# Splitting a projection by columns over two interleaved stages of a four-layer vision kernel

## Chip, cores and metric

The kernel runs on one core of a Trainium2 chip, as one program. The metric is the device time of one execution in microseconds. The time before is 5893.0 us, the median of three runs (5887.95 to 5899.55).

## What is computed

The input x has the shape (8, 56, 56, 192), in float32 throughout. Four layers follow each other, each of the form x = x + layer(groupnorm(x)). Layers 0 and 1 are alike and are the ones that matter here; layer 2 is a depthwise convolution with an MLP, layer 3 a windowed attention. Cut to what matters, with w for the layer's own weights:

```python
x = gn(x)                                  # (8, 56, 56, 192), normalized in 32 groups
p = silu(x @ p_w.T + p_b)                  # 576 channels
q = silu(x @ q_w.T + q_b)
v = silu(x @ v_w.T + v_b)
qv = q * v
o1 = toeplitz(qv along w, a1)              # per channel, a 56 x 56 Toeplitz matrix
o2 = toeplitz(qv along h, a2)
out = (p * (o1 + o2)) @ o_w.T + o_b        # back to 192 channels, added to x
```

The Toeplitz matrices a1 and a2 come from a small MLP over the lags, times a decay. The reference computes these products by FFT; the kernel multiplies by the matrices.

## The kernel before

Samples are held in pairs (j and j + 4), so that there are four pairs; j0 = 0 names the pairs 0 and 1, j0 = 2 the pairs 2 and 3. Each of layers 0 and 1 is made of three generators for each j0:

- Q(i, j0), `tno_qv` (from L223): the projection to q and v, 1152 columns in all, their Silu and their product qv. It walks over 3136 tokens in groups of 256: `load` (L235, issued at L239 on SP's queue) fetches x of two groups ahead, `normalize` (L242, L245 on ScalarE) applies the group norm in place. Each block of 128 tokens is taken against columns 0 to 511, 512 to 1023 and 1024 to 1151 in turn (the loop over c0). `unit` (L253) makes the matmuls (L262), in which x is the loaded weight and the columns of wq move, and adds the bias on VectorE (L271). One unit later `multiply` (L296) makes the Silu (L300, ScalarE) and the product of the q and v halves (L303, GpSimd); its store to qv in HBM (L306, SP's queue) is issued one `multiply` later still. The columns are laid out in blocks of 128, of which the first 64 are q channels and the next 64 the v channels that belong to them, so that column c0 yields the block rows from 2 * c0 / 128 of qv.
- TZ(i, j0), `tno_toeplitz` (from L364): 9 pairs of block rows of qv, each taken along w (d = 0) and along h (d = 1), so 18 rounds. A round loads its part q of qv (L378 or L381) and its matrices tm (L388), both on SP's queue and both double buffered, and makes 8 groups of matmuls (L401), each copied out of PSUM by ScalarE (L408). VectorE transposes (L419, L421), GpSimd adds the second direction (L423) and stores the sum o (L433). The load of round n + 2 is issued at the end of round n. It gives 72 steps of two groups.
- O(i, j0), `tno_out` (from L473): the gate p, its product with o, the output projection, the residual and the statistics of the next group norm. It walks over 28 tiles of 224 tokens of a pair: loads of x (L119) and of o (L498, the tile `t<-L_sum`), normalization (L505), matmuls for p (L526, L535, L561, L563), Silu (L545), the gate on GpSimd (L552, L581), the output matmuls (L568 to L576), residual (L584, L587), a store (GpSimd's queue) and statistics (L590).

The tiles of Q and O come from the same pools, tp with three buffers of each kind: t6 holds x, t8 the projection's result z or O's s, t4 products. Every group of matmuls takes one of four PSUM tiles (`bank`).

The order of the work is written out by hand: within the Toeplitz stages the instructions of every compute engine stand in the order in which the Python code makes them (`manual_schedule`). `weave` (L628) makes that order. It runs a lane, a list of generators each with a cost, one after the other; each yield returns the cost that was just issued. Beside it it draws steps of a Toeplitz generator so that their share of the cost `given` follows the lane's progress:

```python
want = (done / total - lo) / (hi - lo) * given
while steps is not None and gave < want:
    more = next(steps, None)
```

with lo = 0.04 and hi = 0.92. When 0.9 of a generator's cost is done, `weave` starts the first loads of the one that follows; before it starts those of the next weave's lane it draws what is left of the steps. The costs are QT = 298.1 for a Q, OT = 299.6 for an O and TZT = 238.4 for a TZ.

`tno_layers` (L665) lists the lanes at L720 and L721 and runs them in four Toeplitz weaves at L731 and L732:

| weave | lane | Toeplitz steps | from to, us |
|---|---|---|---|
| 1 | Q(0, 2) | TZ(0, 0) | to about 1050 |
| 2 | O(0, 0), Q(1, 0) | TZ(0, 2) | 1050 to 1888 |
| 3 | O(0, 2), Q(1, 2) | TZ(1, 0) | 1888 to 2722 |
| 4 | O(1, 0) | TZ(1, 2) | 2722 to 3297 |

Afterwards O(1, 2) runs beside the first half of layer 2's convolution (L735). The weights wq of Q live in a pool of their own, wqp, which is closed after the third weave.

Of the kernel before, what the change touches and what calls it, by code (L numbers as in the profile page):

```python
# [31 lines left out]
D1 = 576  # L32
# [6 lines left out]
def view(ap, offset, dims):  # L39

    return bass.AP(ap.tensor, ap.offset + offset, [ap.ap[0], *dims])


class Net:
# [175 lines left out]
        for more in self.all_norms():  # L220
            pass

    def tno_qv(self, L, j0, xs, gn, qv, apart=None):  # L223

# [8 lines left out]
        def load(g):  # L235
            t0, n = g * GT, min(GT, T - g * GT)
            x = p.tile([128, 2, 3, GT], F32, name="t6")
            of = xs[j0 : j0 + 2, :, :, t0 : t0 + n].rearrange("j k p t -> p (j k) t")
            nc.sync.dma_start(x[:, :, :, :n].rearrange("p j k t -> p (j k) t"), of)  # L239
            return x, t0, n  # L240

        def normalize(x, t0, n, js=(0, 1)):  # L242
            for j in js:
                for k in range(3):
                    nc.scalar.activation(  # L245
                        x[:, j, k, :n],
                        x[:, j, k, :n],
                        AF.Identity,
                        bias=gn[:, j0 + j, k, 1:2],
                        scale=gn[:, j0 + j, k, 0:1],  # L250
                    )

        def unit(x, s, m, c0, n, z):  # L253


            pps = [(c, min(256, n - c), self.bank2()) for c in range(0, n, 256)]
            for part in range(2):
                for c, k, pp in pps:
                    for j in range(2):
                        for b in range(2):  # L260
                            rows = HALF[b] if part else slice(0, 128)
                            nc.tensor.matmul(  # L262
                                pp[:m, b, 256 * j : 256 * j + k],
                                x[rows, j, 2 if part else b, s : s + m],
                                w[rows, part, c0 + c : c0 + c + k],

                                start=part == 0 and j == 0,
                                stop=part == 1 and j == 1,
                            )
            for c, k, pp in pps:  # L270
                nc.vector.tensor_add(  # L271
                    z[:m, c : c + k, :],
                    view(pp[:m], 0, [[1, k], [256, 4]]),
                    view(bias[:m], c0 + c, [[1, k], [0, 4]]),
                )
# [20 lines left out]
        def multiply(m, n, z, at, c0):  # L296
            k = n // 128
            for f in stores:
                f()
            nc.scalar.activation(z[:m, :n, :], z[:m, :n, :], AF.Silu)  # L300
            prod = p.tile([128, 4, DC * 4], F32, name="t4")
            half = z[:m, :n, :].rearrange("p (n h c) b -> p n h (c b)", h=2, c=DC)
            nc.gpsimd.tensor_mul(prod[:m, :k], half[:, :, 0], half[:, :, 1])  # L303
            n0 = c0 // 128
            stores[:] = [
                lambda: nc.sync.dma_start(  # L306
                    qv[2 * n0 : 2 * n0 + 2 * k, at : at + m, :].rearrange("n t e -> t n e"),
                    prod[:m, :k].rearrange("p n (h e) -> p (n h) e", h=2),
                )
            ]  # L310

        stores = []
        groups = -(-T // GT)
# [4 lines left out]
        if apart:  # L318
            units = []
            for g in range(2):  # L320
                x, t0, n = loaded[g]
                for s in range(0, n, 128):
                    for c0 in range(0, 2 * D1, 512):
                        k = min(512, 2 * D1 - c0)
# [19 lines left out]
        for g in range(2 if apart else 0, groups):  # L344
            x, t0, n = loaded.pop(0)
            for s in range(0, n, 128):
                m = min(128, n - s)
                for c0 in range(0, 2 * D1, 512):
                    k = min(512, 2 * D1 - c0)

                    if late is not None:
                        multiply(*late)
                    if c0 == 512 and s + 128 >= n and g + 1 < groups:
                        normalize(*loaded[0])
                    z = p.tile([128, 512, 4], F32, name="t8")
                    unit(x, s, m, c0, k, z)
                    late = (m, k, z, t0 + s, c0)
                    if c0 == 0 and s == 0 and g + 2 < groups:
                        loaded.append(load(g + 2))
                    yield 5.3 * k / 512  # L360
        multiply(*late)
# [303 lines left out]
    def tno_layers(self, x0, x1, x2, gn, last):  # L665


        tc, nc = self.tc, self.nc
        LS = ("L0", "L1")
        tables = [  # L670

            [self.dram.tile([D1 + 1, 112], F32, name=f"{L}_tab{d}") for d in range(2)]
            for L in LS
        ]
        mats = [
            [self.dram.tile([D1 // 32, 64, 32 * H], F32, name=f"{L}_mat{d}") for d in range(2)]
            for L in LS
        ]
        qvs = {

            j0: self.dram.tile([D1 // 32, 64 * W, 128], F32, name=f"qv{j0}") for j0 in (0, 2)
        }
        o = [self.dram.tile([B // 2, 9, 128, T], F32, name=f"{L}_sum") for L in LS]
        x = (x0, x1, x2)
        with ExitStack() as ctx, ExitStack() as wqp:
            self.wqp = wqp.enter_context(tc.tile_pool(name="wqp", bufs=1, side="right"))
            self.tp = ctx.enter_context(tc.tile_pool(name="tp", bufs=3))
            Q = lambda i, j0, apart=None: self.tno_qv(LS[i], j0, x[i], gn[i], qvs[j0], apart)
            O = lambda i, j0, woven=True: self.tno_out(LS[i], j0, x[i], gn[i], o[i], x[i + 1], gn[i + 1], woven)
            TZ = lambda i, j0: self.tno_toeplitz(j0, mats[i], qvs[j0], o[i])  # L690
            QT, OT, TZT = 25 * 2.25 * 5.3, 28 * 10.7, 8 + 72 * 3.2

            with tc.tile_pool(name="tab", bufs=2) as tab:
                stats = [self.input_stats(x0, gn[0], j, tab) for j in range(4)]
                for more in stats[0]:
                    pass
                first = Q(0, 0, tab)
                next(first)

                for n in range(14):  # L700
                    next(first)
                    next(stats[1], None)
                for more in stats[1]:
                    pass
                for n in range(10):
                    next(first)
                self.decay_tables("L0", tab, tables[0])
                for st in stats[2:]:
                    for more in st:
                        next(first)  # L710
                none = tab.tile([112, 512], F32, name="none", bufs=1)
                nc.gpsimd.memset(none, 0.0)
                for qv in qvs.values():
                    to = qv[:, T:].rearrange("n (p k) e -> p n (k e)", p=112)
                    nc.gpsimd.dma_start(to, view(none, 0, [[0, D1 // 32], [1, 512]]))
                self.decay_tables("L1", tab, tables[1])
                for t in tables:
                    for d in range(2):
                        nc.gpsimd.dma_start(t[d][D1:], none[:1, :112])
                lanes = [[(first, QT - 104.0)], [(Q(0, 2), QT)], [(O(0, 0), OT), (Q(1, 0), QT)]]  # L720
                lanes += [[(O(0, 2), OT), (Q(1, 2), QT)], [(O(1, 0), OT)], [(O(1, 2, False), OT)]]  # L721
                mat = (m for i in range(2) for m in self.expand_tables(tables[i], mats[i]))
                self.weave(lanes[0], mat, lanes[1][0][0], 72.0, 0.0, 0.88)
            in_order = tc.manual_schedule(engines=ENGINES)
            with tc.tile_pool(name="tz", bufs=1) as self.tz, in_order:
                self.tms = []
                for i in range(2):
                    tm = self.tz.tile([128, 32 * H + 8], F32, name=f"tm{i}")
                    nc.gpsimd.memset(tm, 0.0)
                    self.tms.append(tm)  # L730
                for n, tz in enumerate((TZ(0, 0), TZ(0, 2), TZ(1, 0), TZ(1, 2))):  # L731
                    self.weave(lanes[n + 1], tz, lanes[n + 2][0][0], TZT)  # L732
                    if n == 2:
                        wqp.close()
            self.weave(lanes[5], **last())  # L735


# [906 lines left out]
```

## Time and profile before

| | us |
|---|---|
| median of three runs | 5893.0 |
| the profiled execution | 5873.81 |
| its span, from the first to the last instruction | 5872.0 |
| TensorE busy | 5361.4 (91%) |
| VectorE busy | 2362.3 (40%) |
| ScalarE busy | 2267.0 (39%) |
| GpSimd busy | 2209.1 (38%) |
| mean TensorE clock granted | 0.955 |

All lines shown are of that one execution. L262 is line 262 of the kernel. In the page's slices a digit is the busy share of one fortieth of the span in tenths, PEclk is the granted clock of TensorE in tenths of full speed, and DMA is the mean busy share of the 16 DMA engines. In tables by stretch each line gives the stretch, its length, and then for each engine the busy time and in brackets the number of instructions, followed by clock, DMA share and GB/s. In the timeline a line is a run of like instructions: start, length from the first's start to the last's end, engine, line, operation, what is written and read, how many, and in square brackets the engine's idle time before it with what ended it. The hardware records each float32 matmul of the kernel as two. PEld is the weight load, SPq the DMA queue of SP.

### The profile page before, as it was taken

Reading aid. Unit: us, or ns where it says so; the run is one execution under the profiler, and the core shown is the slowest. Engines: PE = TensorE matmul, PEld = TensorE weight load, DVE = VectorE, ACT = ScalarE, POOL = GpSimd, SP = SyncE. Lnnn points to the kernel's source line nnn. Section 1 sums busy time; section 2 is a strip of 40 time slices with the busy share of each in tenths; the row PEclk is TensorE's granted clock in tenths of the full one; section 3 lists DMA queues with packets and bytes.
Section 4 is the critical chain, followed back from the end, with each engine's and each line's share of the span. In section 5 each row is a group of like instructions: output and inputs, shape, how many; then the busy total and the mean of one; then the engine's idle time right before and its main releaser. Section 6 shows DMA issues by size and latency. Waiting matters only on the chain.

```text
span 5872.0 us, 143924 instructions
## 1 busy us (share of the span) xinstructions
PE 5361.4 (91%) x64672; PEld 3891.5 (66%) x64672; DVE 2362.3 (40%) x3770; ACT 2267.0 (39%) x2990; POOL 2209.1 (38%) x1529
## 2 busy tenths in 40 slices
PE   5998888899999999999888799989999999889897
PEld 2776666677777777777666678856665445666665
DVE  6434454233454233553344322331222322555565
ACT  2334454344454444554444322242323333333332
POOL 1334566466456565565666300000001001333332
PEclk8999998999999999999999899999999999999998
DMA  7799997788786788886999566634444223344442
GB/s 267 162 220 264 268 280 238 222 257 273 209 234 213 238 251 230 242 256 191 310 287 303 171 210 207 231 123 155 149 161 120 65 62 62 73 96 84 92 88 59
DMA packets 1139528, 1119.25 MB, mean 191 GB/s; under 512 B 342528, under 2 KB 1076736, under 8 KB 1123488
## 3 DMA queue, kind: packets, MB, share of 16 engines
q1 hardware_dynamic: 1103328, 909.05, 56.8%
q0 software_dynamic: 35584, 200.98, 8.9%
q8 instruction: 508, 8.32, 0.6%
q14 instruction: 108, 0.88, 0.1%
HBM read 753.79 MB, written 389.15 MB: 195 GB/s over the span
## 4 chain that ended last, share of the span: by engine, by line
PE 54%; DMA 11%; POOL 10%; issue 8%; DVE 8%; SPq 6%; ACT 3%; POOLq 0%; DVEq 0%; ACTq 0%
PE bank L262 12%; PE bank L953 6%; POOL s L423 4%; PE bank L814 4%; PE bank L1033 4%; PE bank L401 4%; DMA qv<-t 4%; PE bank L526 4%; PE bank L571 3%; DMA t<-L_sum 3%; PE bank L1047 3%; SPq L378 2%; POOL t L552 2%; SPq L388 2%; POOL t L303 2%
## 5 line engine op out<-in xcount | busy, mean ns | idle before, releaser
L262 PE MATMUL bank<-wq,t 128*128 128x256 f32 (+4 forms) x7680 | 1308.2, 379 | 101.4 <-DVE t L271 50.8
L262 PEld LDWEIGHTS bank<-wq,t 128*128 128x128 f32 (+2 forms) x7680 | 1021.3, 193 | 391.4 <-issue 113.3
L271 DVE TENSOR_TENSOR t<-bank,wq 128x1024 f32<-128x1024 f32 (+3 forms) x480 | 517.3, 1112 | 821.3 <-PE bank L262 559.1
L303 POOL TENSOR_TENSOR t<-t 128x1024 f32<-128x1024 f32 (+2 forms) x288 | 518.9, 1815 | 728.5 <-DMA qv<-t 395.4
L408 ACT COPY ot<-bank 128x896 f32<-128x896 f32 x576 | 492.7, 914 | 643.2 <-PE bank L401 377.1
L423 POOL TENSOR_TENSOR s<-s,ot 128x1568 f32<-128x1568 f32 x144 | 617.9, 4296 | 78.4 <-DVE ot L421 77.7
L401 PE MATMUL bank<-q,tm 56*32 56x224 f32 x18432 | 515.3, 359 | 72.4 <-DMA tm<-L_mat 23.1
L300 ACT ACTIVATE t<-t 128x2048 f32<-128x2048 f32 (+2 forms) x288 | 422.7, 1488 | 407.3 <-DVE t L271 393.1
L401 PEld LDWEIGHTS bank<-q,tm 56*32 56x32 f32 x18432 | 348.8, 107 | 203.8 <-issue 121.0
L552 POOL TENSOR_TENSOR t<-t,t 128x896 f32<-128x896 f32 x168 | 347.2, 2084 | 344.3 <-DMA t<-L_sum 164.3
L526 PE MATMUL bank<-t,wo 128*128 128x224 f32 x1792 | 394.8, 375 | 51.3 <-ACT t L505 22.7
L584 DVE SCALAR_TENSOR_TENSOR t<-bank,wo,t 128x448 f32<-128x448 f32 x112 | 76.4, 682 | 885.7 <-ACT t L580 417.3
L953 PE MATMUL bank<-z,w 128*128 128x448 f32 (+1 forms) x1344 | 417.5, 558 | 3.4 <-ACT h L962 3.4
L526 PEld LDWEIGHTS bank<-t,wo 128*128 128x128 f32 x1792 | 348.2, 201 | 88.5 <-issue 28.6
L545 ACT ACTIVATE t<-bank,wo 128x448 f32<-128x448 f32 x448 | 248.0, 635 | 396.9 <-PE bank L535 368.4
L571 PE MATMUL bank<-t,wo 128*128 128x224 f32 x1792 | 376.2, 364 | 0.0
L127 POOL DMA_DIRECT2D x<-x x64 | 36.7, 573 | 870.1 <-DVE x L984 840.0
L571 PEld LDWEIGHTS bank<-t,wo 128*128 128x128 f32 x1792 | 335.8, 193 | 33.0 <-issue 31.7
L814 PEld LDWEIGHTS bank<-xt,cm 113*112 113x112 f32 x3072 | 314.8, 180 | 45.6 <-issue 38.3
L419 DVE STREAM_TRANSPOSE s<-ot 128x1792 f32<-128x1792 f32 x144 | 292.3, 2034 | 112.2 <-DMA L_sum<-s 65.0
L814 PE MATMUL bank<-xt,cm 113*112 113x108 f32 (+2 forms) x3072 | 326.0, 266 | 8.3 <-ACT h L962 5.1
L953 PEld LDWEIGHTS bank<-z,w 128*128 128x128 f32 (+1 forms) x1344 | 183.7, 190 | 209.6 <-issue 200.2
(149 smaller groups left out, 6984.4 us busy)
## 6 DMA issues: line engine op xcount, KB each, us to landing
q<-qv SPq DMA_DIRECT2D x36, 3584.0 KB
q<-qv SPq DMA_DIRECT2D x72, 1568.0 KB
L_sum<-s POOLq DMA_DIRECT2D x288, 392.0 KB, 7.4
t<-L_sum SPq DMA_DIRECT2D x112, 1008.0 KB
qv<-t SPq DMA_DIRECT2D x192, 512.0 KB
cm<-in_L_cm SPq DMA_DIRECT2D x96, 896.0 KB
tm<-L_mat SPq DMA_DIRECT2D x72, 896.0 KB
x<-t POOLq DMA_DIRECT2D x112, 336.0 KB, 7.1
```

What stands on the lines that cost most here:

```text
L262: nc.tensor.matmul(pp[:m, b, 256 * j : 256 * j + k], x[rows, j, 2 if part else b, s : s + m], w[rows, part, c0 + c : c0 + c + k],  start=p ...
L271: nc.vector.tensor_add(z[:m, c : c + k, :], view(pp[:m], 0, [[1, k], [256, 4]]), view(bias[:m], c0 + c, [[1, k], [0, 4]]),)
L300: nc.scalar.activation(z[:m, :n, :], z[:m, :n, :], AF.Silu)
L303: nc.gpsimd.tensor_mul(prod[:m, :k], half[:, :, 0], half[:, :, 1])
L401: nc.tensor.matmul(pt[32 * j : 32 * j + 32, r, hf * 224 : (hf + 1) * 224], tm[rows, at : at + 32], q[rows, :, 4 * c : 4 * c + 4], start=Tr ...
L408: nc.scalar.copy(view(ot, 4 * (g % 4), [[16, 2], [32, 112], [1, 4]]), view(pt, 0, [[512, 2], [4, 112], [1, 4]]),)
L423: nc.gpsimd.tensor_add(to, to, view(of, 0, [[1, 28], [32, 56]]))
L526: mm(gs[c // 2][:, b, c % 2 * 256 : c % 2 * 256 + N], pw[:, 0, 128 * c : 128 * c + 128], xn[:, b], start=c % 2 == 0, stop=False,)
L552: gate.tensor_mul(to, to, pg)
L571: mm(P[:, b, :N], ow[:, c, 0:128], g[:, 4 * b + c], start=False, stop=c == 3 and b == 1)
L814: nc.tensor.matmul(pc[:, 128 * e + 4 * m0 : 128 * e + 4 * m1], cm[:113, e, k, :], xt[:, m0 - 1 + k : m1 - 1 + k, c + e, :], start=n == 0 a ...
L953: nc.tensor.matmul(phs[c][:, s, :TT], w0[rows, part, at : at + 128], z[rows, Z[2 if part else s], :], start=part == flip, stop=part != flip,)
```

## The change

`tno_qv` gets a range of columns. Its loop over c0 runs over that range only, the place of the normalization of the next group and of the load of the next but one are set by the range, and all else stays. The projection of the second layer for the pairs 2 and 3, Q(1, 2), is made of two generators. The first takes the columns 0 to 511 of all tokens and stays in the third weave, behind O(0, 2). The second takes the columns 512 to 1151, and stands at the head of the fourth weave's lane, ahead of O(1, 0). It loads and normalizes x again. The fourth weave's Toeplitz products TZ(1, 2) are drawn from its beginning, so that their first rounds, on the block rows 0 to 7 of qv, stand beside the second pass, whose own block rows are 8 to 17. The costs given to `weave` are 4/9 and 5/9 of QT. The pool of wq is closed after the fourth weave.

```diff
-    def tno_qv(self, L, j0, xs, gn, qv, apart=None):
+    def tno_qv(self, L, j0, xs, gn, qv, apart=None, cols=(0, 2 * D1)):
...
-                for c0 in range(0, 2 * D1, 512):
-                    k = min(512, 2 * D1 - c0)
+                for c0 in range(*cols, 512):
+                    k = min(512, cols[1] - c0)
...
-                    if c0 == 512 and s + 128 >= n and g + 1 < groups:
+                    if c0 == max(cols[0], min(512, cols[1] - 512)) and s + 128 >= n and g + 1 < groups:
                         normalize(*loaded[0])
...
-                    if c0 == 0 and s == 0 and g + 2 < groups:
+                    if c0 == cols[0] and s == 0 and g + 2 < groups:
                         loaded.append(load(g + 2))
...
-            Q = lambda i, j0, apart=None: self.tno_qv(LS[i], j0, x[i], gn[i], qvs[j0], apart)
+            Q = lambda i, j0, *more: self.tno_qv(LS[i], j0, x[i], gn[i], qvs[j0], *more)
...
-                lanes += [[(O(0, 2), OT), (Q(1, 2), QT)], [(O(1, 0), OT)], [(O(1, 2, False), OT)]]
+                parts = [Q(1, 2, None, cols) for cols in ((0, 512), (512, 2 * D1))]
+                lanes += [[(O(0, 2), OT), (parts[0], QT * 4 / 9)], [(parts[1], QT * 5 / 9), (O(1, 0), OT)]]
+                lanes += [[(O(1, 2, False), OT)]]
...
                     self.weave(lanes[n + 1], tz, lanes[n + 2][0][0], TZT)
-                    if n == 2:
-                        wqp.close()
+                wqp.close()
```

## The prediction

> **What bounds the kernel now.** I read the page's slices first, then cut the timeline at the weaves' boundaries and looked at busy times stage by stage, then at what TensorE waited for, and last at single instructions to get prices.
>
> ```profile
> PE   5998888899999999999888799989999999889897
> PEclk8999998999999999999999899999999999999998
> DMA  7799997788786788886999566634444223344442
> ```
>
> PE is nearly full everywhere, but slices 20 to 22 (2.8 to 3.2 ms) show PE at 8 and DMA at 9: there the transfers hold TensorE back. In the third weave (1888 to 2722 us, output projection O(0,2) and projection Q(1,2) beside the Toeplitz products TZ(1,0)) and the fourth (2722 to 3297 us, O(1,0) beside TZ(1,2)):
>
> ```profile
> core 0: us, PE busy (x) PEld busy (x) DVE busy (x) ACT busy (x) POOL busy (x), PEclk, DMA share, GB/s
> 1888.00:2722.00 834.00, 802.32 (x8899) 616.35 (x8898) 334.81 (x356) 384.64 (x527) 483.07 (x295) 0.98 0.80 236
> 2722.00:3297.00 575.00, 486.72 (x6872) 368.08 (x6872) 205.98 (x226) 240.33 (x374) 364.99 (x226) 0.93 0.93 279
> ```
>
> The third is TensorE's: 96% busy, clock 0.98, DMA with room. The fourth is not: TensorE idles 88 us and its granted clock is 0.93. Cut into three:
>
> ```profile
> 2722.00:2750.00 28.00, 20.65 (x120) 16.18 (x120) 0.68 (x1) 10.29 (x17) 11.94 (x7) 0.82 0.98 202
> 2750.00:3230.00 480.00, 423.83 (x6492) 320.50 (x6496) 188.83 (x199) 216.59 (x334) 303.33 (x191) 0.95 0.97 294
> 3230.00:3297.00 67.00, 42.23 (x280) 31.41 (x259) 16.47 (x26) 13.44 (x24) 49.72 (x29) 0.82 0.58 205
> ```
>
> For 480 us DMA stands at 0.97, so that stretch goes at the transfers' pace; before it lies a start in which O fills its pipeline, after it a tail with no Toeplitz work. Prices come from undisturbed places in the timeline:
>
> ```profile
> 2689.65 32.28 PE L262 MATMUL bank<-wq,t 128*128 128x256 f32 x206
> ...
> 2735.27 6.27 PE L526 MATMUL bank<-t,wo 128*128 128x224 f32 x16 [7.35 <-ACT t L505]
> ...
> 2771.47 3.26 PE L401 MATMUL bank<-q,tm 56*32 56x224 f32 x128
> 2774.65 3.29 PE L526 MATMUL bank<-t,wo 128*128 128x224 f32 x16
> ...
> 2788.32 3.26 PE L401 MATMUL bank<-q,tm 56*32 56x224 f32 x128
> 2791.50 3.10 PE L526 MATMUL bank<-t,wo 128*128 128x224 f32 x15
> ```
>
> From L526 to L526 is 16.85 us with three Toeplitz steps (192 L401 records). A step (64 records) costs 1.6 us (3.18 from start to start for two), so an output tile costs 12.0. 206 records of L262 take 32.28 us; a block of 128 tokens has 80, so 12.5 us; the 512-column part is 32 of its 72 record weights (a 128-wide record counted half), 5.6 us, the other 640 columns 6.9.
>
> **What the Trainium skill says.** "Perfetto Trace Analysis", Optimization Strategy: where a kernel has regimes with different most-contended engines, interleaving them may help. The trace has such regimes, 0.80 and 0.93 of DMA. "TensorE: Matmul & The Clock Gate", What's actually happening: after about 3.4 us of idling the array's clock is gated to half. The trace agrees: after 7.35 us idle, 16 matmuls take 6.27 us, against 3.29 at 2774.65. So a stall costs more than its length. "DMA: Bandwidth & Descriptors", Issuing engines are not separate DMA queues: transfers of SP and POOL share the same 16 engines; so the new loads add to one budget. The 0.97 above is of all queues together, which fits; no run here isolates it.
>
> **The change, part by part.** Work per stage at those prices. O and TZ: 28 tiles x 12.0 + 72 steps x 1.6 = 451 us of TensorE. Q: 25 blocks x 12.5 = 313. So the third weave holds 764 and takes 834 (70 lost), the fourth holds 451 and takes 575 (124 lost).
> DMA, as share times length: fourth 0.93 x 575 = 535 for O and TZ; third 0.80 x 834 = 667, so Q costs 132. Q moves 9.6 MB of x and 28.9 MB of stores; by bytes 33 and 99.
>
> (1) Moved: the 640-column pass, 25 x 6.9 = 174 us of TensorE, from the third weave to the fourth, with its DVE adds, Silus, POOL products, 50 of 75 stores. TensorE after: third 451 + 139 = 590, fourth 451 + 174 = 625. POOL would be 0.6 busy in each, as it is now in the fourth (365/575 = 0.63): not a bound.
> (2) Added: 13 loads of x on SP's queue (9.6 MB) and 78 normalizations (L245) on ACT. 78 of them take 38.67 us in the third weave, so 39 us on an ACT that stays under 0.5 busy. They hide behind TensorE; if the cover is gone they hold back the Silus and PSUM copies behind them. DMA after: third 535 + 33 + 99 x 4/9 = 612; fourth 535 + 33 + 99 x 5/9 = 623.
> (3) Re-dealt: Toeplitz steps. The weave spreads 238 units of cost over 432 instead of 598 in the third, over 465 instead of 300 in the fourth. In the built order an output tile now carries mostly two steps in both, where the third had about 1.5 and the fourth 3. TZ(1,2) begins after three pass-two blocks, with block rows 0 to 7 of qv that pass one wrote; its fifth pair of blocks is loaded right behind the last store of pass two. That load waits for the store; behind it in SP's queue stand a matrix load and O's s and x loads. A store lands in some us, and four Toeplitz steps with the output work between them (about 30 us) lie before its use; I take 0, at most 10.
> (4) Waits added: the first q load of TZ(1,2) waits for pass one's last store, as it did for Q's last store before (2.6 us on SP, once). Stores of pass two queue behind it; three product buffers cover that. Not below nothing: no wait is removed here. Normalizing at the head of pass two stops TensorE for at most a few us; taken as 3.
> (5) Freed: the fourth weave opens with 5 blocks of pure projection, with no filling of O's pipeline (28 us, of which 20 busy). The switch from Q to O comes later in the stage; I keep 10 us for it. The closing of the weight pool later holds nothing: its successors open after the fourth weave.
>
> Times. Third: its last 8% (34 of 432 units) has no Toeplitz work, 36 us; the rest is 555 us of TensorE, against 612 - 20 = 592 of DMA; DMA ends last, at the 0.97 that the full stretch reached: 610. Switches and group norms 15 (now: two waits of 3 us, one of 7 with the half clock behind). 661. Fourth: 5 blocks alone 34; tail of 3.5 tiles 42 plus 25 of what the tail now loses (67 for 2.3 tiles, so 40; a longer tail leaves POOL more time); between, TensorE 549 against DMA 623 - 47 = 576, at 0.97: 594; switches 16. 711. Sum 1372 against 1409 now: -37, rounded to -35. The profiled execution took 5873.8 (span 5872.0 and 1.8 around it), so 5839; it lies 19 under the median, 5893, from which I count: 5858. Later stages keep their order of instructions.
>
> **Rivals.**
> *More gain.* If DMA share is not a rate limit short of 1.03 (it reached 294 GB/s only where 6 MB per tile were asked for), TensorE binds: 590 + 45 and 625 + 65 of losses, 1325: -84, 5809. For it: the third weave ran at 0.86 to 0.89 with TensorE full between 2130 and 2250. Against: two near-full resources seldom mesh.
> *No change.* The share is a conserved sum: 612 + 623 is 33 more than now, and 5% of friction where both are near full (+30) eats the 37. 5893 within 12.
> *Slower.* In pass one, groups of 256 tokens last two units, not two blocks. A load of x stands three units ahead of its normalization, 3 x 8.5 = 26 us, where it stood three blocks and a unit, some 56 us (412/25 = 16.5 a block). It queues behind q loads of 3.5 MB (12 us each at 294 GB/s) and behind SP's waits for q's buffer (up to 19.7 us in the third weave). If it lands late, ACT stands at L245, the PSUM copies behind it stand, TensorE idles and falls to half clock. Over 11 groups 3.3 us each undo the gain; 5 us each give -35 + 55 = +20, 5913. Against: in the third weave L245 is waited for only 0.8 us in all now, and SP's long waits are few.
> *Not doing what it says*: the built order shows the products behind pass one, so no chance.
>
> **Numbers.** Forecast 5858 (between 5833 and 5881): 0.45. More gain: 0.17. No change, within 0.2% (12 us, about what a measurement of this kernel can tell): 0.16. Slower: 0.22. Faster 0.62. The range leaves out half of the big-gain case and of the slow one: 5815 to 5912, from unknown costs of -84 to +20.
>
> **What would show it.** Right: the two weaves sum to some 1372; the fourth's clock rises from 0.93 to about 0.97 and its PE share from 85% to over 90; DMA stands at 0.9 or more in both; L245 doubles by 39 us on ACT and nobody waits for it. Wrong: ACT waiting for t<-x at L245 and TensorE behind it; an output tile of the third weave above 16.5 us; the Q stretch of the third at clock below 0.95, as the projection beside dense products had from 420 to 1050 us (0.90); stalls on q<-qv at TZ's fifth block.

## The result, and the profile after

The changed kernel takes 5866.6 us (median of five runs, 5863.55 to 5869.61) beside 5887.95 for the kernel before (five runs); the ratio is 0.996, with a 95% interval from 0.9946 to 0.9975. That is 21 us less, with an interval of about 15 to 32 us, where 35 were forecast. A later set of runs of the same kernel gave 0.9964 (0.995 to 0.9977).

The slices of the page that were shown of the kernel before:

```profile
PE   5998888899999999999899899989999999988888
PEclk8999999999999999999999899999999999999998
DMA  7799998788786999989897566644444223344442
```

The hole that PE had in slices 20 to 23 (8, 8, 8, 7) is mostly filled (8, 9, 9, 8); DMA is now at 8 or 9 from slice 14 to 21. The boundaries of the weaves moved: the third runs from 1891 to 2556 us, the fourth from 2556 to 3294.

```profile
core 0: us, PE busy (x) PEld busy (x) DVE busy (x) ACT busy (x) POOL busy (x), PEclk, DMA share, GB/s
1891.00:2556.00 665.00, 624.81 (x7704) 471.71 (x7701) 264.80 (x282) 324.52 (x477) 408.62 (x247) 0.96 0.91 270
2556.00:3294.00 738.00, 668.43 (x8075) 507.79 (x8075) 278.98 (x302) 337.18 (x503) 439.83 (x275) 0.95 0.86 253
```

The third weave is 169 us shorter than before (834), the fourth 163 longer (575). The two regimes of DMA, 0.80 and 0.93, have become 0.91 and 0.86. The fourth weave is TensorE's now, at 668 of 738 us, but its clock is only 0.95 and 70 us are idle. Cut by generator, third weave first:

```profile
1891.00:2371.00 480.00, 450.96 (x5753) 340.06 (x5750) 167.10 (x212) 209.69 (x338) 287.78 (x186) 0.96 0.94 273
2371.00:2556.00 185.00, 173.85 (x1952) 131.65 (x1952) 97.70 (x70) 114.84 (x140) 120.84 (x61) 0.98 0.83 263
2556.00:2811.00 255.00, 234.99 (x2800) 180.73 (x2800) 118.67 (x97) 136.55 (x177) 124.45 (x74) 0.95 0.89 243
2811.00:3294.00 483.00, 433.44 (x5279) 327.06 (x5275) 160.30 (x206) 200.63 (x326) 315.38 (x202) 0.95 0.84 259
```

These are O(0,2), the first pass, the second pass and O(1,0). The second pass has TensorE busy for 235 of 255 us. What TensorE waited for in the fourth weave, in us, times and the longest:

```profile
PE bank L568 <- POOL t L581: 23.7, 6, 11.9
PE bank L561 <- ACT t L545: 14.2, 2, 14.0
PE bank L401 <- DVE t L271: 10.5, 3, 5.3
PE bank L262 <- DVE t L271: 8.8, 6, 5.3
PE bank L78 <- DVE gn_mv L71: 6.7, 2, 3.7
PE bank L262 <- ACT t L245: 4.2, 1, 4.2
```

The first line is mostly the tail of the output projection, which the kernel before has too, in its fourth weave:

```profile
PE bank L568 <- POOL t L581: 22.6, 2, 11.4
```

The next three lines are new in this weave: TensorE waits for the bias adds L271 of the second pass, and once for 14 us for ScalarE's L545. Following them back among the waits of all engines from 2556 to 2840 us:

```profile
POOL t L303 <- DMA qv<-t: 101.1, 14, 20.6
DVE t L271 <- POOL t L303: 76.7, 17, 9.9
...
ACT t L545 <- DMA qv<-t: 14.4, 1, 14.4
```

GpSimd's product L303 waits 101 us for the store of an earlier product to free its buffer, VectorE's L271 then waits for the buffer z that L303 still reads, and TensorE for L271. The kernel before has the wait for stores too, in its third weave, where the projection stood:

```profile
POOL t L303 <- DMA qv<-t: 80.3, 11, 16.0
```

In the changed kernel it comes to 129.1 us in weaves 3 and 4, of which 101.1 lie beside the second pass and at its end. The 14 us are the same wait, at the switch to the output projection. The timeline shows it:

```profile
2814.88 1.78 PE L535 MATMUL bank<-t,wo 64*128 64x224 f32 x16
...
2815.42 16.41 SPq L306 DMA_DIRECT2D qv<-t  x3
...
2816.59 1.74 PE L401 MATMUL bank<-q,tm 56*32 56x224 f32 x64
...
2830.51 0.71 POOL L303 TENSOR_TENSOR t<-t 64x256 f32<-64x256 f32 x1 [8.53 <-DMA qv<-t]
2831.15 1.16 ACT L545 ACTIVATE t<-bank,wo 128x448 f32<-128x448 f32 x2 [14.37 <-DMA qv<-t]
...
2832.36 1.01 PE L561 MATMUL bank<-t,wo 128*64 128x224 f32 x4 [14.02 <-ACT t L545]
...
2834.66 3.24 PE L401 MATMUL bank<-q,tm 56*32 56x224 f32 x64 [0.34 <-ACT t L545]
```

O's gate (L545) writes into a t4 buffer, which the last products of the projection still hold until their stores land. Just ahead of the stall 64 matmul records of L401 take 1.74 us, and behind it 3.24: TensorE runs at about half its pace for a while, as it did behind the 7.35 us of idling in the prediction's lines.

### The profile page after: what moved, and what is told of

The parts are those of the page before. It is cut to its first block, busy times and chain, and to the rows that moved or that the text cites. A ratio compares the mean times of both kernels' runs of the same rounds, so it can differ in the third digit from the quotient of the medians.

```text
span 5861.8 us, 144059 instructions
## 1 busy us (share of the span) xinstructions
PE 5365.4 (92%) x64672; PEld 3886.4 (66%) x64672; DVE 2363.8 (40%) x3770; ACT 2304.9 (39%) x3068; POOL 2209.3 (38%) x1529
## 4 chain that ended last, share of the span: by engine, by line
PE 55%; POOL 12%; DMA 11%; SPq 7%; DVE 7%; issue 5%; ACT 2%; POOLq 0%; DVEq 0%; ACTq 0%
PE bank L262 9%; PE bank L954 6%; DMA qv<-t 6%; PE bank L815 5%; POOL s L423 5%; PE bank L1034 4%; PE bank L571 4%; PE bank L526 4%; PE bank L401 3%; SPq L388 3%; DMA t<-L_sum 3%; PE bank L1048 3%; SPq L378 2%; POOL t L303 2%; POOL t L552 2%
## 5 line engine op out<-in xcount | busy, mean ns | idle before, releaser
L271 DVE TENSOR_TENSOR t<-bank,wq 128x1024 f32<-128x1024 f32 (+3 forms) x480 | 517.0, 1111 | 836.0 <-PE bank L262 524.2
L303 POOL TENSOR_TENSOR t<-t 128x1024 f32<-128x1024 f32 (+2 forms) x288 | 519.0, 1815 | 786.3 <-DMA qv<-t 457.0
L401 PE MATMUL bank<-q,tm 56*32 56x224 f32 x18432 | 522.5, 361 | 64.4 <-DVE t L271 18.8
L401 PEld LDWEIGHTS bank<-q,tm 56*32 56x32 f32 x18432 | 345.0, 108 | 205.4 <-issue 96.1
L552 POOL TENSOR_TENSOR t<-t,t 128x896 f32<-128x896 f32 x168 | 347.6, 2087 | 323.1 <-DMA t<-L_sum 208.8
L526 PE MATMUL bank<-t,wo 128*128 128x224 f32 x1792 | 388.7, 371 | 27.4 <-ACT t L505 18.1
L545 ACT ACTIVATE t<-bank,wo 128x448 f32<-128x448 f32 x448 | 248.2, 635 | 404.7 <-PE bank L535 356.3
L526 PEld LDWEIGHTS bank<-t,wo 128*128 128x128 f32 x1792 | 343.9, 198 | 64.1 <-issue 30.5
```

What stands on the lines that cost most here:

```text
L271: nc.vector.tensor_add(z[:m, c : c + k, :], view(pp[:m], 0, [[1, k], [256, 4]]), view(bias[:m], c0 + c, [[1, k], [0, 4]]),)
L401: nc.tensor.matmul(pt[32 * j : 32 * j + 32, r, hf * 224 : (hf + 1) * 224], tm[rows, at : at + 32], q[rows, :, 4 * c : 4 * c + 4], start=Tr ...
L526: mm(gs[c // 2][:, b, c % 2 * 256 : c % 2 * 256 + N], pw[:, 0, 128 * c : 128 * c + 128], xn[:, b], start=c % 2 == 0, stop=False,)
L552: gate.tensor_mul(to, to, pg)
```

## Experiments

The theory: the gain comes from evening the Toeplitz transfers over more TensorE work, and what is missing of the forecast is lost to late stores of the second pass. Rivals: the second load of x eats the gain; the DMA engines are simply full; or the weaves gain nothing and the difference lies elsewhere. To compare weaves, all lengths in the table are taken between the first matmuls of the generators, up to the group norm behind O(1,0), in us; each line is one profiled execution.

| kernel | O(0,2) | Q or pass 1 | pass 2 | O(1,0) | weaves 3 and 4 |
|---|---|---|---|---|---|
| before | 436 | 398 | | 576 | 1410 |
| before, again | 433 | 397 | | 580 | 1410 |
| changed | 480 | 185 | 255 | 483 | 1402 |
| changed, again | 478 | 186 | 255 | 481 | 1400 |
| changed, own small buffers | 479 | 185 | 241 | 474 | 1378 |
| changed, own small buffers in pass 2 only | 478 | 185 | 246 | 467 | 1377 |
| before, own small buffers | 432 | 389 | | 581 | 1402 |
| changed, own small buffers, late products | 478 | 185 | 185 | 581 | 1429 |
| split alone (both passes in weave 3) | 436 | 404 for both | | 574 | 1414 |
| before, stores on GpSimd's queue | 442 | 391 | | 583 | 1415 |
| changed, stores on GpSimd's queue | 479 | 186 | 243 | 483 | 1390 |
| changed, both remedies | 480 | 186 | 239 | 477 | 1383 |
| changed, more transfers | 498 | 188 | 256 | 481 | 1422 |
| cut at 768, stores on GpSimd's queue | 465 | 248 | 187 | 541 | 1441 |

**Both kernels again.** No edit.

> The changed kernel once more, for a second profile. Evening theory (the gain comes from spreading the Toeplitz transfers over more TensorE work): 0.996 of before again (about -21 us), third weave near 664 us and fourth near 741, with stalls of TensorE in pass two and at the switch to the output projection. Rival (the two stages gain nothing, as 1409 against 1405 us in the one pair of profiles says, and the medians differ for another reason, such as the stages behind): the sum of the two weaves is within 5 us of 1409 again.

It measured 0.9964 of before; the weaves 1400 us.

> The kernel before once more, for a second profile. Its first profiled execution (5873.8 us) lay at the lower end of its runs, and by that pair of profiles the third and fourth weave gained 8 us only (1410 against 1402), where the medians gained 21. If the gain lies in these weaves, a profile near the median shows them at 1415 to 1425; if they stay at 1410, the rest of the 21 us is spread over other stages and is noise of single executions.

One execution of 5885.5 us; the weaves 1410 us again. So two profiles of each agree: the third and fourth weave gain 8 to 10 us, and about half of the 21 us of the medians lies in them. The rest is not located: behind the weaves, where the order of instructions is the same, the two pairs differ by 6 us on average, ahead of them by 4 the other way. The rival that the weaves gain nothing is wrong, but for these two kernels it stays open where the other half of the 21 us comes from.

**The split alone.** Both passes in the third weave:

```diff
-                lanes += [[(O(0, 2), OT), (parts[0], QT * 4 / 9)], [(parts[1], QT * 5 / 9), (O(1, 0), OT)]]
+                lanes += [[(O(0, 2), OT), (parts[0], QT * 4 / 9), (parts[1], QT * 5 / 9)], [(O(1, 0), OT)]]
```

> Both passes stay in the third weave, behind each other, so x is loaded and normalized twice but nothing is moved to the fourth. Evening theory: the fourth weave is back at 575 us; the third has 33 us more of DMA on 667 in 834, which hides, so it stands at 834 to 845; in all 0 to +10 us against before. Rival (splitting itself helps, for instance because stores of 512 columns are all of one size): 10 us or more faster than before. Rival (the second load eats the gain): 20 us or more slower than before.

Measured: 5883.2 us, 0.9988 (0.9978 to 0.9999), 5 us less in the medians, just below the 0 to +10 that was expected. In the one profile weaves 3 and 4 are 4 us longer than before (1414), and the two passes take 404 us where the whole projection took 398, with DMA at 0.87 in place of 0.74. So the second load and normalization cost a few us at most where DMA has room, and splitting without moving is hardly worth anything.

**Small products in buffers of their own.** In `multiply`, where the products of 128 columns get two small buffers, and in `tno_out`, whose tile t1 becomes a second user of them:

```diff
-            prod = p.tile([128, 4, DC * 4], F32, name="t4")
+            prod = p.tile([128, 4, DC * 4], F32, name="t4") if k == 4 else p.tile([128, 1, DC * 4], F32, name="t1", bufs=2)
...
-                pg = p.tile([128, N], F32, name="t1", bufs=1)
+                pg = p.tile([128, 256], F32, name="t1", bufs=2)[:, :N]
```

> The changed kernel, but the products of the 128-column units go to two small buffers of their own, so that the three large ones serve only 512-column units. Theory of late stores (in pass two each block makes two stores and GpSimd waits for the stores' buffers, TensorE behind it): waits of L303 for qv stores fall from 129 us in the two weaves to under 70, the fourth weave loses 10 to 20 us, in all -10 to -20 against the changed kernel. Rival (the DMA engines are full and a buffer only moves the wait): within 5 us of the changed kernel.

It measured 0.982 (0.9803 to 0.9837), 5782.6 us: far more than either expected, since the wait stands in every projection beside Toeplitz products. L303's waits for stores from 500 to 3300 us, before, in the changed kernel, and with small buffers:

```profile
POOL t L303 <- DMA qv<-t: 295.5, 40, 20.8
...
POOL t L303 <- DMA qv<-t: 352.5, 50, 21.0
...
POOL t L303 <- ACT t L300: 330.4, 71, 21.6
...
POOL t L303 <- DMA qv<-t: 102.3, 16, 16.0
```

In weaves 3 and 4 alone they fall from 129.1 to 55.8, as expected. L303 waits mostly for its input now. The edit also gives O's tile a second buffer; that this alone gains nothing is seen at O(0,2), where no projection runs beside it and whose length stays (478 to 480 us in the changed kernel, 479 here). The fourth weave went from 737 to 715 us, 14 of it in pass two and 9 at and behind the switch.

**The same on the kernel before.**

> The kernel before, with the products of the 128-column units in two small buffers of their own, as in the run on the changed kernel (0.982 of before there). Theory of late stores (the buffers' wait stands in every projection beside Toeplitz products, and splitting the projection spread it over two weaves): weaves 1 and 2 gain the 44 and 18 us they gained there, the third 5 to 15, in all -65 to -80 us; the split is then worth 10 to 25 us on top. Rival (the split and the buffers help each other, since the second pass has twice the share of small stores): at most -60 us, and the split is worth 25 us or more on top.

Measured: 0.9882 (0.9864 to 0.99), 5816.3 us. With small buffers on both sides the split is worth 0.982 against 0.9882: 34 us in the medians, 24 in the weaves (1402 against 1378). With three shared buffers it is worth 21 and 9. The medians' intervals are too wide to tell 34 from 21; the weaves are not, where two profiles of one kernel differ by 3 us at most. So the split and the late stores do interact, as the rival had it, though the buffers alone gave the kernel before more (68 us) than the rival allowed.

**Small buffers in the second pass only.** The same edit with `if k == 4 or not cols[0]`.

> The changed kernel with small buffers of their own for the 128-column products of the second pass only; the three other projections keep the three shared buffers. Theory of late stores (what the split earned less than forecast was lost in pass two and at the switch behind it): only the fourth weave changes, from 737 to about 715 us, weaves 3 and 4 together near 1379, in all about -20 to -25 us against the changed kernel (0.992 to 0.993 of before). Rival (the fourth weave ran shorter with small buffers everywhere because the earlier weaves shifted what meets what): weaves 3 and 4 stay within 8 us of 1401.

Measured: 0.993 (0.9914 to 0.9946), 5843.8 us; weaves 3 and 4 together 1377. The third weave is 663 us, the fourth:

```profile
2548.00:2794.00 246.00, 234.68 (x2801) 179.93 (x2800) 119.74 (x97) 138.11 (x179) 128.32 (x79) 0.95 0.95 258
2794.00:3261.00 467.00, 432.34 (x5272) 327.51 (x5272) 158.11 (x205) 198.20 (x324) 311.24 (x196) 0.96 0.86 265
```

The same TensorE work (235 and 432 us busy) ends in 714 in place of 737 us, 9 of them gained in pass two and 15 in O(1,0), where the stall at the switch is gone: L545 no longer waits for a store. O(0,2) has the second buffer of `tno_out` here too and stays at 478. What the change lost in the fourth weave against the forecast is thereby shown to be the buffers that the second pass's small stores held. The transfers are the same as in the changed kernel, so the DMA engines were not simply full.

**Stores on GpSimd's queue.** The store L306 is issued by `nc.gpsimd`, on the changed kernel and on the one before.

> The changed kernel with the qv stores of all projections issued on GpSimd's queue in place of SP's, so that they stand behind no q load in SP's queue and SP doesn't wait for products. Theory of late stores behind q loads: the 16 us stall at the switch to the output projection goes, GpSimd waits less for stores, 15 to 40 us faster than the changed kernel over all four projections. Rival (GpSimd's issue time, some 0.5 to 1 us for each of 300 stores, and its own queue cost as much): same or slower by up to 20 us.

> The kernel before with the qv stores issued on GpSimd's queue, as in the run on the changed kernel (0.982 of before there, weaves 3 and 4 together 1390 us). Theory of late stores: about as much as the small buffers give, -60 to -80 us. Rival (what it takes away is the switch inside the fourth weave, which the kernel before does not have): -50 us or less.

Measured: 0.982 (0.9806 to 0.9834) and 0.9873 (0.9857 to 0.9889), 30 us apart. It helps as much as the buffers do, again mostly in the earlier weaves. The expected end of the switch's stall did not come: TensorE still waits 15.6 us there for L545, and L545 for a store. Weaves 3 and 4 measured 1390 and 1415 us, so here too the split is worth 25 us in them.

**Both remedies.**

> The changed kernel with both: small buffers of their own and qv stores on GpSimd's queue. Theory of late stores (both remove the same wait): within 10 us of either alone (0.982 of before). Rival (two causes, too few buffers and SP's queue): 0.972 or less.

Measured: 0.9803 (0.9788 to 0.9819), 5774.1 us, the fastest version of all. The 8 us more than either alone are within the intervals, so the two gain hardly more together than each alone: both remove the same wait.

**More transfers.** Each load of x in the two passes followed by a copy of the same x to an unused place in HBM.

> The changed kernel with each load of x in its two passes followed by a copy of the same x to another place in HBM: 19 MB more of transfers on the same queue, used by nothing. Theory that DMA binds both weaves (the price of the prediction, 33 us for 9.6 MB): +40 to +70 us against the changed kernel, and the 9.6 MB that the change adds cost it 20 to 33. Rival (single waits bind, not the sum of transfers): under +20 us.

Measured: 5888.7 us, 1.0005 of before, 22 us more than the changed kernel; its weaves 3 and 4 are 1422, also 22 more. So 19.3 MB cost 22 us, between the two expectations. But SP's queue is not in the order written by hand: all 26 copies, those of pass two as well, were issued between 2177 and 2406 us, most beside O(0,2), which went from 480 to 498 us with DMA at 0.98, and none beside pass two. There the transfers bind. In proportion 9.6 MB would cost 11 us; that is an estimate, and what the change's own loads cost beside the passes, where DMA stands at 0.83 and 0.89, was not measured.

**Toeplitz products begun after the second pass.** On the kernel with small buffers, the fourth weave's `lo` is 0.36 in place of 0.04:

```diff
-                    self.weave(lanes[n + 1], tz, lanes[n + 2][0][0], TZT)
+                    self.weave(lanes[n + 1], tz, lanes[n + 2][0][0], TZT, 0.36 if n == 3 else 0.04)
```

> The changed kernel with small buffers of its own for the 128-column products (0.982 of before), but the Toeplitz products of the fourth weave begin only when its second pass is done, so that they stand beside the output projection at three steps a tile as before the change; the projection's move to the fourth weave stays. Evening theory: the output tiles of the fourth weave go back from about 16 to about 20 us, the second pass runs alone at TensorE's pace (174 us); the fourth weave gets 15 to 40 us longer, of the 35 us that the split is worth there a third or less is left. Rival (only the third weave's relief counts, or the dense products of the fourth weave have hidden slack): within 8 us of the kernel with small buffers.

Measured: 0.9903 (0.9885 to 0.992), 5835.5 us, 53 more than with early products (0.982), beyond the 15 to 40 that were expected. Weaves 3 and 4 are also 27 us longer than in the kernel before with small buffers, which has no split (1402); the medians of these two, 19 us apart, have intervals that overlap. Second pass and O(1,0):

```profile
2498.00:2684.00 186.00, 185.45 (x1201) 148.34 (x1201) 75.39 (x74) 97.13 (x130) 75.28 (x49) 0.98 0.64 180
2684.00:3264.00 580.00, 494.44 (x6874) 369.91 (x6872) 204.14 (x228) 240.31 (x374) 365.04 (x226) 0.92 0.89 265
```

Alone, the second pass runs at TensorE's pace; O(1,0) is back at its 580 us of before the change, clock 0.92. So moving the pass is worth nothing by itself: the whole gain hangs on the products that are spread over it. This is the clearest evidence for the evening theory.

**Another cut.** Passes of 768 and 384 columns, costs 6/9 and 3/9, with stores on GpSimd's queue; the next group is normalized at the first unit of a block of tokens.

> Stores on GpSimd's queue as in the run with 0.982, but the projection cut at column 768 in place of 512: passes of 768 and 384 columns, costs 6/9 and 3/9. TensorE then has 660 us in the third weave and 555 in the fourth (590 and 625 at the cut of 512), DMA 635 and 602. Evening theory: the fourth weave is held by DMA again, its tiles above 16 us; 5 to 20 us slower than the cut at 512 with the same stores. Rival (the place of the cut doesn't matter, each moved us counts once): within 5 us.

Measured: 0.9906 (0.9891 to 0.992), 5832.2 us, 50 more than the cut at 512 with the same stores, far more than expected, and 21 more than no split at all with the same stores (5811.3 us; weaves 3 and 4 1415 against 1441 here). The third weave, which is given more work, is 49 us longer than with the cut at 512 (714 against 665); the fourth, which is given less, is no shorter (728 against 725): O(1,0) takes 541 us in place of 483, though DMA's share in that stretch is only 0.83. Its products stand at 2.3 steps a tile (cost 238.4 / (0.88 x 399), times 10.7 for a tile, divided by 3.2 for a step), against 1.95. From 2735 to 3135 us GpSimd waits 84 us for O's s tile (L552 for `t<-L_sum`, up to 20 us each) and ScalarE 46 us for GpSimd, against 63 and 8 with the cut at 512. So the place of the cut decides whether the split gains or loses, but the mean DMA share does not show why: it is 0.88 in that stretch with either cut, and yet loads of s are waited for longer with the one. That these late loads are the cause is argued; which wait starts it was not tried.

## Why the prediction was right, and where it was off

**The bound of the kernel before, and the direction:** right. The fourth weave was held by transfers, and spreading its steps over a projection pass is what gains, as the late products show (+53 us).

**The total** came out right in part by luck. Of the 37 us that were forecast for weaves 3 and 4, the profiles show 8 to 10: 1372 forecast, 1402 and 1400 measured, 1378 once the late stores are gone. The measured 5866.6 us lie 26 under the 5893 from which the forecast counted: 5 of them are the kernel before itself, which five runs put at 5887.95, 8 to 10 are the weaves, and the remaining 11 to 13 were not forecast and are not located.

**The third weave**, forecast 661: measured 665. Within it the sign set for an output tile was passed: 480/28 = 17.1 us with group norms and starts, where above 16.5 was to count as wrong. A tile in the quiet stretch takes 15.3 (from L526 at 2289.95 to the next at 2305.28); events make up the rest. The first pass took 185. The 0.97 of DMA that was to set the pace was nearly reached beside O(0,2) (0.94) and not beside the pass (0.83); TensorE is 94% busy, so both are near their limits, and what sets the pace there was not separated.

**The fourth weave**, forecast 711: measured 737, and this is where the prediction failed. The step is (4), "three product buffers cover that". They did not: a block of the second pass makes two products and two stores, one of them of 128 columns, each holding one of three buffers until it lands, and the stores stand with the q loads in SP's queue. Small buffers in that pass alone bring the fourth weave to 714. A second part of the same error is in (5): of the 25 us of the switch from projection to output (2811 to 2836) TensorE is busy for 10.4, so 14.6 are lost where 10 were kept for it, nearly all in the 14 us stall on a t4 buffer. The kernel before had shown the wait for stores, 80.3 us in the third weave, and the prediction gave it no cost.

**TensorE's price** was low too. Alone, the second pass keeps TensorE busy for 185 us (late products), where 174 were priced, and the fourth weave as a whole for 668, where 625 were summed (before: 487, where 451 were). DMA has 0.86 x 738 = 635 us of work there, close to the 623 forecast. TensorE's time contains stretches at a lower clock (0.95 on the mean). So in the fourth weave TensorE is the longer of the two, and not DMA, as the sum had it; the length with small buffers, 714, lies near to 711, but it is made up differently.

**The added loads and normalizations**, (2): 9.6 MB priced at 33 us of DMA by bytes. Their cost in time was not measured alone where they stand; the copies suggest some 11 us where transfers bind (an estimate in proportion), and the split alone a few at most. ScalarE gained 38 us (77.35 us of L245 in both weaves, 38.67 before). TensorE waited 8.5 us for L245, and L245 itself waited for no load: the slower rival's mechanism did not occur. (Its 412 us for the projection before are 398 between first matmuls, 15.9 us a block in place of 16.5; nothing hangs on it.)

**The clock** of the fourth weave was to rise from 0.93 to about 0.97; it rose to 0.95. PE's share is 668/738 = 91%, as forecast; DMA is 0.86, below the 0.9 named, but the forecast's own sum gives only 623/711 = 0.88. The clock of the projection in the third weave is 0.98, and TensorE waits for no q load in the fourth: these two signs of being wrong did not come.

**Between two cases:** the measured time lies between the forecast and the rival of no change, whose reason (friction where two resources are near full) named the effect but not the place.

## What to carry to other kernels

When a stage is made denser, count the buffers that are held until a store lands, and not only the bytes of the stores: a small tile in a pool of large buffers takes a whole one, as here a product of 128 KB took the place of one of 512 KB. A wait that costs nothing in one arrangement may cost in the next; before moving work beside it, ask what its slack is. And a mean DMA share below 1 does not say that single transfers come in time.

## What the runs showed of the hardware

Moving 300 stores from SP's queue to GpSimd's gained as much as two extra buffers (0.9873 and 0.9882 on the kernel before): on GpSimd's queue a store of 512 KB lands in 7.5 us (median on the kernel before, from 500 to 3300 us), and a product waited at most 7.3 us for a store, where on SP's queue it waited up to 21. The stall at the switch in the changed kernel stayed with the other queue (15.6 us) and went with the extra buffers. Which part of it is the transfers' order in the queue and which is SP's own waiting ahead of a store was not separated.
